# Turning token blocks through DRAM and VectorE in three stages, and dealing PSUM banks anew in a fourth

## The chip, the cores and the metric

One core of a Trainium2 chip runs the whole program. The metric is the device time of one execution in microseconds (us); the time of a kernel is the median of its runs.

## The reference

A decoder of two layers on x, 16 blocks of 128 tokens by 512 features, in float32. Each of the six parts is followed by an add and a layer norm:

```python
x = ln(x + attention(x))               # layer 0: 16 heads of 32, 4 key heads, rotary, softmax
x = ln(x + cross_attention(x, ctx))    # layer 0: low-rank queries and keys, context of 128 x 128 a block
x = ln(x + ffn(x))                     # layer 0: (sigmoid(x w1) * (x w2)) w3, weights cut to -1, 0, 1
x = ln(x + decay_attention(x))         # layer 1: scores times a decay, no softmax
x = ln(x + cross_attention_1(x, ctx))  # layer 1: softmax with a causal mask
x = ln(x + experts(x))                 # layer 1: 2 of 8 experts a token, and a shared one
```

A projection `x @ w` needs the tokens with their features on the partitions, that is, each block of x turned from (128 tokens, 512 features) to four squares of (128 features, 128 tokens). How the blocks are turned is what this case is about.

## The kernel before

All of x lies in SBUF as 16 tiles `x[b]` of 128 tokens by 512 features. The stages run one after the other; each goes through the blocks in four groups of four (`GB` = 4, `NG` = 4), and projects a whole group of 512 tokens at a time from a turned tile `xT` (128 features x 4 x 512 tokens).

The kernel deals with eight banks of PSUM, each large enough for 128 x 512 float32. `psum.share(mm=..., sc=..., ...)` shares them out by name for a stage, and `bank("mm", ...)` takes the next one of that name; a bank is free again when the last reader of its tile is done.

Before the change a block is turned in one way only in these stages: four TensorE transposes into a `mm` bank (`transpose_x`, records L127), and one copy out of it by ScalarE (L128). The FFN has its own form of it (L663), since it splits the turned block into a high and a low part, `xh` by ScalarE (L664) and `xl` by VectorE (L665).

- **First attention** (`attend` with its `prepare`, `score`, `value`). While group g is attended, the tasks of `prepare(g + 1)` are dealt in parts (`Share`) between the softmax pieces: four `turn`s, 20 projection matmuls, the values, and for g >= 2 a `folds` task that multiplies two heads' weights of the next stage together, out of a tile `raw` loaded from DRAM (two buffers). For g = 4 four more folds follow, of which the first can start when an earlier fold has freed its `raw`.
- **Cross-attention of layer 0** (`context`, `project`, `Heads`; banks mm=2, sc=4, av=2). 32 steps, one for each block and half of the heads. A step takes two `sc` banks for its scores (L563); VectorE finds the maximum (L186), ScalarE takes Exp with eight instructions (L191), GpSimd scales. Then the probabilities are turned by way of DRAM: VectorE's transpose turns 32 x 32 squares (L580), SP writes the tile to DRAM (L584) and fetches it in four DMAs that set the squares in place (L587). Two steps later `out` multiplies with `mT` into one `mm` bank, `po` (L605), which VectorE adds to x (L610). At a group's start `context` turns context and tokens (`pk` L531, `tr` L127), and `project` makes `qT` and `kT` (L546, L549), all through `mm`. Between the steps VectorE also sums and cuts the FFN's weights (`piece`, L470, L497, L499).
- **FFN** (`inputs`, then 11 steps f for each group; banks mm=2, sc=3, pt=2, av=1). A step is 16 matmuls into `pa` and `pb` (L687), a sigmoid (L692), a product `ht` on VectorE (L694), its high part `hh` (L696) and low part `hl` (L698). One task of the list `todo` is run ahead of each step but the first: in group 0 the cuts of the third weight's last pieces, then the next group's blocks to turn.
- **Decay attention** (banks mm=2, sc=4, av=2). A group's four blocks are turned, 8 x 4 projection matmuls follow (L775), the values (L783), and then the blocks go through a pipeline of three stages: scores (L799), values (L814), output (L148).

The order of instructions on each engine is settled when the program is built: a scheduler reckons with costs and takes, of what is ready, what was written first. `keep_in_program_order` pins an instruction behind everything that was written before it for its engine. A queue then runs in that order, and an instruction that waits holds all behind it; this is so for SP, which issues nearly all DMAs, too. Two buffers of a tag (`bufs=2`) let the writer run one tile ahead of the reader.

Of the kernel before, what the change touches and what calls it, by code (L numbers as in the profile page):

```python
# [12 lines left out]
F32 = mybir.dt.float32  # L13
F32R = mybir.dt.float32r
AF = mybir.ActivationFunctionType
ALU = mybir.AluOpType
AX = mybir.AxisListType

P = 128
# [26 lines left out]
def decoder_kernel(ctx: ExitStack, tc: tile.TileContext, a: dict, out: bass.AP):  # L46
# [25 lines left out]
    def bank(tag, shape, name):  # L72
        return psum.pool.tile(shape, F32, tag=tag, name=name, bufs=psum.banks[tag])
# [18 lines left out]
    def load_x(b0, b1):  # L92
        for b in range(b0, b1):
            nc.sync.dma_start(x[b], a["x"][b])
# [28 lines left out]
    def transpose_x(xT, b, at):  # L123

        tr = bank("mm", [P, KC, P], "tr")
        for k in range(KC):
            nc.tensor.transpose(tr[:, k, :], x[b][:, k * P : (k + 1) * P], ident)  # L127
        nc.scalar.copy(xT[:, :, at : at + P], tr)  # L128

    def chain(tasks, name, pairs, then):  # L130

# [179 lines left out]
    with tc.tile_pool(name="p1", bufs=1) as p1:  # L311
# [47 lines left out]
                    nc.vector.tensor_tensor(br, br, b2, ALU.add)  # L359

        load_x(GB, NB)
        LATE = H // 2 - 2
        nc.sync.dma_start(wkr, a["l0x_wkr"])
        hd = DC // 2
# [30 lines left out]
        def prepare(g):  # L395
            if g == NG:
                room = p1.tile([P, KC, TG], F32, tag="xT", name="room")
                ct, t2 = (room[:, n].rearrange("p (b d) -> p b d", d=DC) for n in range(2))
                return [(0, rotate(0, ct, kvr0, t2))] + folds(2, LATE)
            xT = p1.tile([P, KC, TG], F32, tag="xT", name="xT")  # L400
            qkT = p1.tile([P, 5, TG], F32, tag="qkT", name="qkT", bufs=2)
            v = p1.tile([P, GB, P], F32, tag="v", name="v", bufs=2)
            groups[g] = qkT, v
            tasks = []

            def turn(i):
                transpose_x(xT, g * GB + i, i * P)
                nc.gpsimd.tensor_tensor(x[g * GB + i], x[g * GB + i], bo, ALU.add)

            tasks += [(0.64, lambda i=i: turn(i)) for i in range(GB)]  # L410
            for c in range(5):
                chain(
                    tasks, "pq", [(wr[:, k, c * P : (c + 1) * P], xT[:, k, :]) for k in range(KC)],
                    lambda pq, c=c: nc.scalar.activation(qkT[:, c, :], pq, AF.Identity, bias=br[:, c : c + 1]),  # L414
                )
            got = {}

            def values_in(i):
                if i == 0:
                    got["pv"] = bank("pt" if g == 0 else "mm", [P, GB, P], "pv")  # L420
                for k in range(KC):
                    nc.tensor.matmul(
                        got["pv"][:, i, :], lhsT=xT[:, k, i * P : (i + 1) * P], rhs=wv[:, k, :],
                        start=(k == 0), stop=(k == KC - 1),
                    )
                if i == GB - 1:
                    nc.vector.tensor_tensor(v, got["pv"], bc(bv, GB), ALU.add)

            vals = [(0.93, lambda i=i: values_in(i)) for i in range(GB)]
            if g == 0:  # L430
                tasks = [t for pair in zip(tasks, vals) for t in pair] + tasks[GB:]
            else:
                tasks += vals
            return tasks + (folds(g - 2, g - 1) if g >= 2 else [])

# [63 lines left out]


    with tc.tile_pool(name="p2", bufs=1, reuse_waits="tile") as p2:
        psum.share(mm=2, sc=4, av=2)


        tern = Ternary(p2)
# [145 lines left out]
    with tc.tile_pool(name="p3", bufs=1) as p3:  # L653
        w1, w2 = (tern.w[n].rearrange("p (k f) -> p k f", k=KC) for n in range(2))
        def inputs(g):
            xh = p3.tile([P, KC, TG], F32R, tag="xh", name="xh", bufs=2)
            xl = p3.tile([P, KC, TG], F32R, tag="xl", name="xl", bufs=2)

            def one(i):
                at = slice(i * P, (i + 1) * P)  # L660
                tr = bank("mm", [P, KC, P], "tr")
                for k in range(KC):
                    nc.tensor.transpose(tr[:, k, :], x[g * GB + i][:, k * P : (k + 1) * P], ident)  # L663
                nc.scalar.copy(xh[:, :, at], tr)  # L664
                nc.vector.tensor_tensor(xl[:, :, at], tr, xh[:, :, at], ALU.subtract)  # L665
            return (xh, xl), [lambda i=i: one(i) for i in range(GB)]

        xs, todo = inputs(0)
        for run in todo:
# [4 lines left out]
        for g in range(NG):  # L674
# [2 lines left out]
                coming, more = inputs(g + 1)  # L677
                todo += more
            for f in range(NF0):
                if f and todo:  # L680
                    todo.pop(0)()
                pa = bank("sc", [P, TG], "pa")
                pb = bank("pt", [P, TG], "pb")
                for dst, wt in ((pa, w1), (pb, w2)):
                    for k in range(KC):
                        for n in range(2):
                            nc.tensor.matmul(  # L687
                                dst, lhsT=wt[:, k, f * P : (f + 1) * P], rhs=xs[n][:, k, :],
                                start=(k == 0 and n == 0), stop=(k == KC - 1 and n == 1),
                            )  # L690
                sg = p3.tile([P, TG], F32, tag="sg", name="sg", bufs=2)
                nc.scalar.activation(sg, pa, AF.Sigmoid)  # L692
                ht = p3.tile([P, TG], F32, tag="ht", name="ht", bufs=2)
                nc.vector.tensor_tensor(ht, sg, pb, ALU.mult)  # L694
                hh = p3.tile([P, TG], F32R, tag="hh", name="hh", bufs=NF0 + 1)
                nc.scalar.copy(hh, ht)  # L696
                hl = p3.tile([P, TG], F32R, tag="hl", name="hl", bufs=NF0 + 1)
                nc.gpsimd.tensor_tensor(hl, ht, hh, ALU.subtract)  # L698
                hs.append((hh, hl))
# [26 lines left out]
    with tc.tile_pool(name="p4", bufs=1) as p4:  # L726
# [28 lines left out]


        pipe = Pipeline((0, 1, 2))
        for g in range(NG):
            xT = p4.tile([P, KC, TG], F32, tag="xT", name="xT", bufs=2)
            for i in range(GB):  # L760
                transpose_x(xT, g * GB + i, i * P)
                nc.gpsimd.tensor_tensor(x[g * GB + i], x[g * GB + i], bo4, ALU.add)
            if g == 0:
                for j in range(4):
                    dj = p4.tile([P, 4, P], F32, tag=f"dec{j}", name=f"dec{j}")
                    for c in range(4):
                        h = 4 * c + j
                        nc.scalar.activation(dj[:, c, :], diff, AF.Exp, scale=nsl[:, h : h + 1])
                    nc.gpsimd.tensor_tensor(dj, dj, bc(maskT, 4), ALU.mult)
                    dec.append(dj)  # L770
            qkT = p4.tile([P, 8, TG], F32, tag="qkT", name="qkT", bufs=2)
            for c in range(8):
                pq = bank("mm", [P, TG], "pq")
                for k in range(KC):
                    nc.tensor.matmul(  # L775
                        pq, lhsT=wq4[k // 2][:, k % 2, c * P : (c + 1) * P], rhs=xT[:, k, :], start=(k == 0), stop=(k == KC - 1)
                    )
                nc.scalar.activation(qkT[:, c, :], pq, AF.Identity, bias=bcol[:, c : c + 1])
            vs = []
            for i in range(GB):  # L780
                pv = bank("mm", [P, D], "pv")
# [5 lines left out]
                v = p4.tile([P, D], F32, tag="v", name="v", bufs=6)  # L787
                nc.vector.tensor_tensor(v, pv, bv4, ALU.add)
                vs.append(v)
            for i in range(GB):  # L790
                toks = slice(i * P, (i + 1) * P)
                mine = {}

# [626 lines left out]
```

## Time and profile before

| | |
|---|---|
| median of 3 runs | 2102.32 us (2101.36 to 2102.72) |
| the profiled execution | 2102.39 us |
| its span, first to last instruction | 2100.6 us |
| TensorE busy | 2038.5 us (97%) |
| VectorE, ScalarE, GpSimd busy | 853.1, 625.0, 646.8 us |
| mean DMA rate | 113 GB/s over the span |

The profile is of one execution. In its rows PE is TensorE's matmul, PEld its weight load, DVE VectorE, ACT ScalarE, POOL GpSimd and SP SyncE, whose only work is issuing DMAs. L127 is line 127 of the kernel. A row of the waits has who waited, for whom, the total in us, the number of waits and the longest. A row of the timeline has the start, the duration, the instruction and, in brackets, the idle time before it. A float32 matmul of 512 columns shows as two records, a transpose as one. A matmul's record lasts longer than the distance to the next one's start, since matmuls are pipelined.

### The profile page before, as it was taken

What the parts mean: (1) busy time and instruction counts of PE and PEld (TensorE: products, weight loads), DVE (VectorE), ACT (ScalarE), POOL (GpSimd) and SP (SyncE); (2) the same over time, 40 slices, a digit from 0 to 9 for tenths busy, and PEclk for the clock granted to TensorE, in tenths of its full rate; (3) what the DMA queues carried; (4) which work ended last, traced back from release to release, by engine and by line L of the source; (5) the groups of instructions that cost most, each with busy time, mean ns of one, the idle gap of its engine ahead of it and who ended that gap; (6) DMA issues with size and microseconds to landing.
All of it is one profiled execution on the core that took longest, in us unless ns stands there. A gap on an engine that the chain in (4) does not pass through costs nothing. (4 is left out here: it accounts for less than half of the span.)

```text
span 2100.6 us, 25187 instructions
## 1 busy us (share of the span) xinstructions
PE 2038.5 (97%) x9221; PEld 1125.7 (54%) x9221; DVE 853.1 (41%) x1728; ACT 625.0 (30%) x2103; POOL 646.8 (31%) x674
## 2 busy tenths in 40 slices
PE   8999989999999999999999999999899999999997
PEld 5555544444444458888555444555544455545552
DVE  4667732444554243222123213777731122232324
ACT  3655532333333222222211111766632200000002
POOL 5555530111211122223223123455613212222223
PEclk9999999999999999999999999999999999999999
DMA  6001231334432220000300008600003379999974
GB/s 230 1 35 40 106 129 54 99 124 125 136 119 78 70 85 1 1 1 35 120 1 1 1 6 248 244 22 21 26 19 126 122 218 305 295 295 305 289 236 165
DMA packets 117067, 238.19 MB, mean 113 GB/s; under 512 B 28752, under 2 KB 73168, under 8 KB 110288
## 3 DMA queue, kind: packets, MB, share of 16 engines
q1 hardware_dynamic: 102048, 129.72, 19.1%
q0 software_dynamic: 13792, 105.55, 15.3%
q8 instruction: 73, 1.20, 0.2%
q10 hardware_dynamic: 1104, 1.31, 0.2%
q14 instruction: 50, 0.41, 0.1%
HBM read 172.25 MB, written 64.30 MB: 113 GB/s over the span
## 5 line engine op out<-in xcount | busy, mean ns | idle before, releaser
L198 POOL TENSOR_TENSOR p<-p,rs 128x512 f32<-128x512 f32 x192 | 200.0, 1043 | 504.8 <-DVE rs L197 500.0
L605 PE MATMUL po<-mT,cc 128*128 128x512 f32 x512 | 232.5, 602 | 3.7 <-ACT cc L598 3.7
L191 ACT ACTIVATE p<-t,nmx 128x128 f32<-128x128 f32 x512 | 198.5, 390 | 34.6 <-POOL p L198 8.8
L605 PEld LDWEIGHTS po<-mT,cc 128*128 128x128 f32 x512 | 95.5, 191 | 117.7 <-issue 107.4
L191 ACT ACTIVATE p<-sc,nmx 128x128 f32<-128x128 f32 x256 | 90.0, 372 | 113.7 <-DVE nmx L186 107.9
L546 PE MATMUL pq<-xT,wqr 128*128 128x512 f32 x256 | 117.9, 602 | 3.0 <-ACT xT L128 3.0
L114 POOL TENSOR_SCALAR ve<-mv 128x1 f32<-128x1 f32 x80 | 18.1, 226 | 324.3 <-DVE mv L112 312.3
L148 PE MATMUL po<-wo,oT 128*128 128x512 f32 x256 | 116.8, 599 | 0.4 <-ACT qkT L414 0.4
L1163 ACT ACTIVATE rsg<-rg 128x352 f32<-128x352 f32 x39 | 18.1, 463 | 331.2 <-PE rg L1158 331.2
L775 PE MATMUL pq<-xT,wq 128*128 128x512 f32 x256 | 110.9, 594 | 1.0 <-ACT xT L128 0.7
L1158 PE MATMUL rg<-ew,xsT 128*128 128x352 f32 x312 | 100.5, 465 | 11.3 <-DMA ew<-in_l1f_w_dram,which 10.6
L1179 PE MATMUL ry<-ew,ractT 128*128 128x512 f32 (+1 forms) x234 | 106.9, 592 | 0.0
L121 POOL TENSOR_SCALAR x<-x,mv,rstd 128x512 f32<-128x512 f32 x48 | 100.6, 2095 | 4.5
L1158 PE MATMUL ru<-ew,xsT 128*128 128x352 f32 x312 | 98.7, 459 | 0.0
L1129 POOL DMA_INDIRECT ew<-in_l1f_w_dram,which x39 | 38.0, 975 | 190.7 <-PE ry L1179 167.9
L191 ACT ACTIVATION_READ_ACCUMULATOR p<-t,nmx 128x1 f32 x512 | 96.2, 188 | 0.0
L698 POOL TENSOR_TENSOR hl<-ht,hh 128x512 fp32r<-128x512 f32 x44 | 60.4, 1372 | 114.9 <-ACT hh L696 114.9
L205 DVE COPY pT<-pt 128x512 f32<-128x512 f32 x128 | 86.5, 679 | 18.0 <-PE pt L203 18.0
L1189 POOL DMA_INDIRECT sums<-ry,place x39 | 62.0, 1590 | 96.2 <-DMA sums<-ry,place 43.9
L203 PEld LDWEIGHTS pt<-ident,p 128*128 128x128 f32 x512 | 59.8, 141 | 53.8 <-issue 44.8
L1041 PE MATMUL pg<-xT,sw_gu 128*128 128x512 f32 x192 | 86.5, 593 | 0.0
L186 DVE TENSOR_REDUCE nmx<-t 128x4 f32<-128x512 f32 x128 | 83.8, 675 | 0.8
(231 smaller groups left out, 3617.7 us busy)
## 6 DMA issues: line engine op xcount, KB each, us to landing
piece<-in_l0f_w_dram SPq DMA_DIRECT2D x48, 352.0 KB
away<-sq SPq DMA_DIRECT2D x32, 512.0 KB
pT<-away SPq DMA_DIRECT2D x128, 128.0 KB
raw<-in_l0x_raw_dram SPq DMA_DIRECT2D x8, 1728.0 KB
slots_x<-zero SPq DMA_DIRECT2D x1, 10023.0 KB
sums<-zero SPq DMA_DIRECT2D x1, 9984.0 KB
xs<-slots_x SPq DMA_DIRECT2D x156, 64.0 KB
sums<-x SPq DMA_DIRECT2D x16, 256.0 KB
```

The lines of the kernel that those rows point to most:

```text
L121: engine.tensor_scalar(x[b], x[b], mean, rstd, ALU.subtract, ALU.mult)
L148: nc.tensor.matmul(po, lhsT=oT[:, c, :], rhs=wo[:, c, :], start=(c == 0), stop=(c == KC - 1))
L186: nc.vector.tensor_reduce(nmx, src, axis=AX.X, op=ALU.max, negate=True)
L191: nc.scalar.activation(self.p[:, j, :], src[:, j, :], AF.Exp, bias=nmx[:, j : j + 1], accum_out=self.sm[:, j : j + 1])
L198: nc.gpsimd.tensor_tensor(self.p, self.p, spread(rs, P), ALU.mult)
L205: nc.vector.tensor_copy(self.pT, pt)
L546: nc.tensor.matmul(pq, lhsT=wqr[:, k, cols], rhs=xT[:, k, :], start=(k == 0), stop=(k == KC - 1))
L605: nc.tensor.matmul(self.po, lhsT=self.cc[:, 4 * par + j, :], rhs=mT[h], start=(par == 0 and j == 0), stop=(par == 1 and j == 3),)
L775: nc.tensor.matmul(pq, lhsT=wq4[k // 2][:, k % 2, c * P : (c + 1) * P], rhs=xT[:, k, :], start=(k == 0), stop=(k == KC - 1))
L1041: nc.tensor.matmul(dst, lhsT=sw_gu[:, k, at : at + P], rhs=xTs[g][:, k, :], start=(k == 0), stop=(k == KC - 1),)
L1158: nc.tensor.matmul(dst, lhsT=self.xT[:, k, :], rhs=gu[:, k, off : off + FE], start=(k == 0), stop=(k == KC - 1),)
L1179: nc.tensor.matmul(po, lhsT=self.actT[:mw, m_, :], rhs=dn[:mw, m_, :], start=(m_ == 0), stop=(m_ == 2))
```

## The change

A new class `Turn` turns a block without TensorE. `send` lets ScalarE regroup x[b] by squares of 32 features into `xp` and writes it to a DRAM tile `turned`; `fetch` brings it back in four DMAs so that the 32 x 32 squares stand where they belong; `back` lets VectorE transpose the squares into `xT`.

- In the first attention, groups 2 and 3: no `send`; eight DMAs, after the loads of x, regroup the input from DRAM to DRAM in runs of 32 floats. The folds of these groups now come ahead of the projections, with the four turns (at cost 0) between them.
- In the FFN, groups 1 to 3: sends and backs go into `todo` in a fixed order, and the list is spread over the steps, so that in group 0 more than one task can fall to a step.
- In the decay attention, groups 1 to 3: two blocks of the next group are sent during the projections, two at the first attention step; they come back at the first and the third. `xT` has one buffer in place of two.
- In the cross-attention of layer 0: four `mm` banks in place of two, two `sc` banks in place of four.

```diff
+    turned = dram.tile([NB, P, D], F32, tag="turned", name="turned")
+    QP = P // 4
+
+    class Turn:
+        def __init__(self, b):
+            self.b = b
+
+        def send(self, pool, tag="xp"):
+            xp = pool.tile([P, 4, KC, QP], F32, tag=tag, name="xp")
+            nc.scalar.copy(xp, x[self.b].rearrange("p (k q a) -> p q k a", k=KC, q=4))
+            nc.sync.dma_start(turned[self.b], xp.rearrange("p q k a -> p (q k a)"))
+
+        def fetch(self, pool, tag="x2", bufs=1):
+            self.x2 = pool.tile([P, 4, P], F32, tag=tag, name="x2", bufs=bufs)
+            rows = turned[self.b].rearrange("(t r) (q f) -> q r t f", r=QP, q=4)
+            for q in range(4):
+                nc.sync.dma_start(self.x2[q * QP : (q + 1) * QP], rows[q])
+
+        def back(self, xT):
+            tc.keep_in_program_order(nc.vector.transpose(
+                xT.rearrange("p k (t r) -> p t k r", r=QP), self.x2.rearrange("p t (k a) -> p t k a", k=KC)
+            ))
@@ first attention, after the loads of x
         load_x(GB, NB)
+        for g in range(2, NG):
+            blocks = slice(g * GB, (g + 1) * GB)
+            for k in range(KC):
+                nc.sync.dma_start(
+                    turned[blocks].rearrange("n p (q k a) -> (n p) q k a", q=4, k=KC)[:, :, k, :],
+                    a["x"][blocks].rearrange("n p (k q a) -> (n p) k q a", q=4, k=KC)[:, k],
+                )
@@ first attention, prepare(g)
             def turn(i):
-                transpose_x(xT, g * GB + i, i * P)
+                if g < 2:
+                    transpose_x(xT, g * GB + i, i * P)
+                else:
+                    mine = Turn(g * GB + i)
+                    mine.fetch(p1, bufs=3)
+                    mine.back(xT[:, :, i * P : (i + 1) * P])
                 nc.gpsimd.tensor_tensor(x[g * GB + i], x[g * GB + i], bo, ALU.add)
 
-            tasks += [(0.64, lambda i=i: turn(i)) for i in range(GB)]
+            tasks += [(0.0 if g >= 2 else 0.64, lambda i=i: turn(i)) for i in range(GB)]
...
-            return tasks + (folds(g - 2, g - 1) if g >= 2 else [])
+            first = folds(g - 2, g - 1) if g >= 2 else []
+            for i in range(GB):
+                first.insert(2 * i, tasks[i])
+            return first + tasks[GB:]
@@ cross-attention of layer 0
-        psum.share(mm=2, sc=4, av=2)
+        psum.share(mm=4, sc=2, av=2)
@@ FFN, inputs(g)
+            turns = [Turn(g * GB + i) for i in range(GB)]
+
+            def sent(i):
+                turns[i].send(p3)
+                turns[i].fetch(p3, bufs=2)
+
             def one(i):
                 at = slice(i * P, (i + 1) * P)
-                tr = bank("mm", [P, KC, P], "tr")
-                for k in range(KC):
-                    nc.tensor.transpose(tr[:, k, :], x[g * GB + i][:, k * P : (k + 1) * P], ident)
+                if g == 0:
+                    tr = bank("mm", [P, KC, P], "tr")
+                    for k in range(KC):
+                        nc.tensor.transpose(tr[:, k, :], x[i][:, k * P : (k + 1) * P], ident)
+                else:
+                    tr = p3.tile([P, KC, P], F32, tag="xT", name="xT")
+                    turns[i].back(tr)
                 nc.scalar.copy(xh[:, :, at], tr)
                 nc.vector.tensor_tensor(xl[:, :, at], tr, xh[:, :, at], ALU.subtract)
-            return (xh, xl), [lambda i=i: one(i) for i in range(GB)]
+
+            if g == 0:
+                return (xh, xl), [lambda i=i: one(i) for i in range(GB)]
+            order = [(sent, 0), (sent, 1), (one, 0), (sent, 2), (one, 1), (sent, 3), (one, 2), (None, 0), (one, 3)]
+            return (xh, xl), [lambda f=f, i=i: f and f(i) for f, i in order]
@@ FFN, the steps of a group
-                if f and todo:
+                for _ in range(-(-len(todo) // (NF0 - f)) if f else 0):
                     todo.pop(0)()
@@ decay attention
+        coming = []
+
+        def send4(b):
+            coming.append(Turn(b))
+            coming[-1].send(p4)
+            coming[-1].fetch(p4, bufs=2)
+            nc.gpsimd.tensor_tensor(x[b], x[b], bo4, ALU.add)
+
         for g in range(NG):
-            xT = p4.tile([P, KC, TG], F32, tag="xT", name="xT", bufs=2)
-            for i in range(GB):
-                transpose_x(xT, g * GB + i, i * P)
-                nc.gpsimd.tensor_tensor(x[g * GB + i], x[g * GB + i], bo4, ALU.add)
             if g == 0:
+                xT = p4.tile([P, KC, TG], F32, tag="xT", name="xT")
+                for i in range(GB):
+                    transpose_x(xT, i, i * P)
+                    nc.gpsimd.tensor_tensor(x[i], x[i], bo4, ALU.add)
...
                 nc.scalar.activation(qkT[:, c, :], pq, AF.Identity, bias=bcol[:, c : c + 1])
+                if c in (2, 4) and g + 1 < NG:
+                    send4((g + 1) * GB + c // 2 - 1)
...
+            if g + 1 < NG:
+                xT = p4.tile([P, KC, TG], F32, tag="xT", name="xT")
             for i in range(GB):
+                if i in (0, 2) and g + 1 < NG:
+                    for n in (i, i + 1):
+                        coming.pop(0).back(xT[:, :, n * P : (n + 1) * P])
+                        if i == 0:
+                            send4((g + 1) * GB + 2 + n)
```

## The prediction

> **What bounds the kernel now.** I read the page first, then busy times by stage, then TensorE's waits, then the timeline at a few places. The page:
>
> ```profile
> PE 2038.5 (97%) x9221; PEld 1125.7 (54%) x9221; DVE 853.1 (41%) x1728; ACT 625.0 (30%) x2103; POOL 646.8 (31%) x674
> PE   8999989999999999999999999999899999999997
> DMA  6001231334432220000300008600003379999974
> ```
>
> TensorE is busy nearly everywhere; DMA is nearly idle in slices 2 to 4 (52 to 210 us) and in the FFN and decay stages. A busy TensorE can hide lost pitch, so I also ask for the four stages that the change touches (first attention, cross-attention, FFN, decay attention):
>
> ```profile
> 0.00:262.00 262.00, 251.90 (x1571) 146.87 (x1571) 167.93 (x337) 140.83 (x577) 144.10 (x147) 0.99 0.23 82
> 262.00:759.00 497.00, 483.94 (x1630) 228.08 (x1628) 203.39 (x381) 160.38 (x628) 93.66 (x109) 1.00 0.32 102
> 759.00:1013.70 254.70, 251.22 (x1124) 206.85 (x1123) 86.36 (x140) 63.04 (x105) 72.84 (x76) 0.99 0.07 24
> 1013.70:1286.00 272.30, 269.67 (x1599) 134.05 (x1598) 75.68 (x132) 46.30 (x81) 67.20 (x73) 1.00 0.14 35
> ```
>
> Columns: stretch, length, busy PE, weight load, DVE, ACT, POOL, granted clock, DMA share, GB/s. TensorE is at 96 to 99% in all four, VectorE at 64, 41, 34 and 28%. So work taken off TensorE counts in full, and VectorE has room. TensorE's waits, the rows that bear on the change:
>
> ```profile
> PE po L605 <- ACT cc L598: 3.7, 1, 3.7
> PE pq L546 <- ACT xT L128: 3.0, 4, 0.8
> PE tr L127 <- DVE x L610: 2.9, 2, 1.8
> PE av L593 <- DMA pT<-away: 1.6, 1, 1.6
> PE tr L127 <- ACT kvT L533: 0.5, 1, 0.5
> ```
>
> All five lie in cross-attention. In the third and fifth the transposes wait for a bank of `mm`, of which there are two there: one held by `po` until VectorE has added it to x (L610), one by `pk`.
>
> **What a transposed block costs TensorE.** FFN timeline:
>
> ```profile
> 907.63 0.39 PE L687 MATMUL pb<-xl,ffn_w 128*128 128x512 f32 x1
> 907.86 0.60 PE L663 MATMUL tr<-ident,x 128*128 128x128 f32 x4
> 908.22 0.48 PE L687 MATMUL pa<-xh,ffn_w 128*128 128x512 f32 x1
> 908.53 0.40 PE L687 MATMUL pa<-xl,ffn_w 128*128 128x512 f32 x1
> ```
>
> The FFN's matmuls start 0.226 us apart (907.63 to 907.86). With four transposes and one matmul between, 907.86 to 908.53 is 0.67, so the four cost 0.67 - 0.226 = 0.44 us. Elsewhere the same: four records last 0.60, one alone 0.272, so they start (0.60 - 0.272)/3 = 0.109 apart, 0.44 for four.
>
> **Transposes removed.** First attention, groups 2 and 3: 8 blocks. FFN, groups 1 to 3: 12. Decay, groups 1 to 3: 12. 32 x 0.44 = 14.1 us (3.5, 5.3, 5.3), all on the engine that sets the end. The small waits beside them (0.24 to 0.34 us at the first attention's group starts, some 0.1 per decay group) give another 0.5.
>
> **What replaces them.** On VectorE one `back` per block. The nearest rows are the same instruction on the same 128x512 tile, 711 ns at L580 and 697 ns at L1147: 0.70. First attention gets 8 x 0.70 = 5.6 us more on 168 of 262; the FFN 8.4 on 86 of 255; decay 8.4 on 76 of 272. The cover is VectorE's idle time; where it is gone, a `back` costs at most its 0.70. In the first attention the four stand in the first third of a group's share instead of being spread, with VectorE at 64%: I charge 0.5 us there (bounds 0 and 5.6).
>
> ScalarE: decay loses 12 copies out of PSUM (L128, 585 ns) and gains 12 copies into `xp` (the row of such a regrouping copy, L1108, has 618 ns): level. The first attention loses 8. The FFN gains 12 x 0.62 = 7.4 on 63 of 255. Free. `xh` and `xl` read SBUF in place of PSUM; L665 at 690 and L696 at 621 (SBUF to SBUF) say at most 0.03 each.
>
> DMA and SP: per block of FFN and decay one write of 256 KB and four fetches. The same pair in cross-attention:
>
> ```profile
> 412.26 0.34 SPq L584 DMA_DIRECT2D away<-sq  x1
> 414.97 1.74 SPq L587 DMA_DIRECT2D pT<-away  x4
> ```
>
> The write is answered 2.71 us after its issue, and the four fetches take 1.74 to issue. With a copy of 0.62 before and a landing that I bound by 1 and 2.7 (as long as the write), a trip takes 6.1 to 7.8 us. While SP waits for the write, everything behind it waits: in the FFN's group 0 the third weight's pieces. A FFN step is 16 x 0.226 = 3.6 us; groups 1 and 2 leave two steps (7.2) from send to `back`. Group 0 leaves one for its first block, but the copy needs only x, so it can run ahead; and `back` on VectorE holds `ht`, for which two `pb` banks give about 4 us of cover. In group 0 two `cut`s per step instead of one make 2 x (0.58 + 0.95) + 0.69 = 3.75 us of VectorE per 3.6 us step for three steps, and pieces 2.9 us from issue to use come two by two: `ht` falls some 2 us behind, inside that cover. I charge 1.0 for the FFN (bounds 0 and 4).
>
> Decay: blocks 0 and 1 of the next group leave during the projections, over 20 us before their `back`; blocks 2 and 3 have two attention steps (scores start 5.75 apart, 1127.15 and 1132.90), 11.5 us, for two trips that share one `xp`: 2 x 4.45 + 0.6 + 1 to 2.7 = 10.5 to 12.2. About even; 0 charged, bounds 0 and 3 x 0.7 = 2.
>
> DRAM to DRAM in the first attention: 8 copies on SP after the last x load (issued until 23.1 us), before `wkr`, the tables and the first two `raw`. See the second rival.
>
> **Banks in cross-attention.** With four `mm` banks the waits for a bank, 2.9 + 0.5, should go: 3.4 us. The 3.0 us in which `pq` waits for the last copy of xT stay: five ScalarE copies of 0.59 still follow one another. `sc` falls from four banks to two: scores of the next block wait for the Exp of this one. The steps are 10 us apart, and the closest case in the trace is this:
>
> ```profile
> 545.06 1.16 PE L563 MATMUL sc<-kT,qT 64*128 64x128 f32 x16
> 552.95 0.37 ACT L191 ACTIVATE p<-sc,nmx 128x128 f32<-128x128 f32 x1
> 553.22 0.48 PE L563 MATMUL sc<-kT,qT 64*128 64x128 f32 x2
> ```
>
> The last Exp ends at 553.32, 0.1 after the next scores start. In the other steps 0.7 to 5 us lie between, so two banks nearly suffice: 0 charged. At the start of the stage four blocks' scores are now done ahead, and ScalarE runs their Exps before the first `cc` (the 3.7 us wait); with two banks it could get to `cc` sooner. Bounds: 0 and a gain of 3.7 plus 1.7 (the granted clock is 0.51 for 3.5 us after that wait: 3.5 x 0.49). I take 0, since nothing shows the new order.
>
> **Sum.** -14.1 - 0.5 - 3.4 + 0.5 + 1.0 = -16.5. The profiled execution took 2102.39 us (span 2100.6), 0.07 from the median of the runs, so the same sum serves: 2102.4 - 16.5 = 2085.9, say 2086. Taking every bound for it (-14.1 - 0.5 - 3.4 - 3.0 - 5.4): 2076.
>
> **Rival 1: the squares come late.** Trips as long as their upper bound and no copy ahead: the FFN's first block 4.2 late, decay 2, and a wait that long is followed by a slow clock, 1.7: about 8 back, so 2094. For it: SP and VectorE keep their order, and one late block holds all behind. Against: x is ready long before. Chance 0.21, nearly all still faster.
>
> **Rival 2: the early copies hold up `raw`.** 2 MB in runs of 32 floats are 8 x 2048 = 16,384 pieces. By bytes, 4.2 MB read and written at the 410 GB/s of the stretch from 16 to 36 us take 10 us; at the mean of the hardware queue's packets (19.1% of 16 x 2100.6 us over 102,048 packets, 63 ns), 16,384 x 63/16 = 64 us. The loads before them end near 36, so they end between 46 and 100, and the first `raw` some 5 us later. The folds now come first in group 2, near 87 us, where the work of group 2 starts in the trace, and not at 136.9. At the upper end TensorE waits 105 - 87 = 18 us: 2104. I take the low end: the mean packet has 1,270 bytes, ten times these, and DMA is idle from 40 to 86 us. The Trainium skill ("DMA: Bandwidth & Descriptors", Specifications) speaks against such pieces: under 512 B a DMA engine reads, modifies and writes. By an estimate from it, twice the bytes' time, they would end near 56, which leaves the sum as it is; no row here shows 128-byte writes to DRAM. Chance 0.07, over half of it within the bound of no change.
>
> **Rival 3, slower: two score banks set the pace of cross-attention.** Of the 32 steps some 24 follow another block's scores directly. If the order, made for banks that free at a reckoned time, puts scores 1.2 us before the Exps are done, 24 x 1.2 = 29 us are lost: 2086 + 29 = 2115. It decides from 16.5/24 = 0.7 us a step. For it: the case above, 0.1 short, and VectorE's sums over the weights, which come between scores and Exp. Against: the median step has about 4 us to spare. Chance 0.09.
>
> **How the numbers follow.** Forecast 0.63 (2076 to 2092), rival 1 0.21 (2090 to 2099), rival 2 0.07, rival 3 0.09. A measurement of this kernel can tell about 0.2%, 4.2 us, from no change. Faster: 0.63 + 0.19 = 0.82; same: 0.02 + 0.04 = 0.06; slower: 0.03 + 0.09 = 0.12. The range 2075 to 2100 holds the forecast with its bounds and rival 1, and leaves out the other two.
>
> **What would show it.** L127 has 320 - 80 = 240 records and L663 16; VectorE has 32 more stream transposes of 0.70; FFN and decay shrink by 4 to 6 us each, first attention by 3, cross-attention by 3 to 4; no wait of `tr` on L610 is left in it. Wrong: waits of `pc` on a `raw` load near 87 us, of `sc` on Exp in cross-attention, or of `ht` on `piece` or on a fetched block.

## The result, and the profile after

The changed kernel takes 2084.76 us (median; 2083.01 to 2086.05) beside 2102.30 (2101.36 to 2102.72) of the kernel before: a ratio of 0.9908, interval 0.9894 to 0.9923. The forecast was 2086.0. The profiled execution took 2083.65 us, its span is 2081.9. The page of the kernel after:

```profile
PE 2024.5 (97%) x9093; PEld 1119.0 (54%) x9093; DVE 880.7 (42%) x1760; ACT 627.3 (30%) x2107; POOL 644.5 (31%) x674
PE   8999999999999999999999999999899999999997
DMA  9200331334432231001410028400004279999974
```

TensorE has 128 instructions fewer (9221 to 9093: 32 blocks of four transposes) and 14.0 us less busy time; VectorE has 32 more instructions and 27.6 us more; 32 `back`s at 0.695 us are 22.2 of them, and where the rest lies is told under FFN below. DMA, idle before in the slices of FFN and decay, now has a few tenths there. The same four stretches as in the prediction:

```profile
0.00:257.50 257.50, 247.31 (x1539) 142.16 (x1539) 172.01 (x345) 136.77 (x569) 144.27 (x147) 0.99 0.33 100
257.50:750.20 492.70, 485.18 (x1630) 233.86 (x1629) 203.65 (x381) 159.94 (x628) 93.71 (x109) 0.99 0.32 103
750.20:999.00 248.80, 245.32 (x1077) 202.17 (x1076) 102.62 (x153) 69.45 (x117) 69.88 (x76) 0.99 0.16 50
999.00:1265.10 266.10, 263.39 (x1551) 130.44 (x1550) 82.80 (x144) 46.55 (x81) 67.57 (x72) 0.99 0.21 60
```

VectorE (the fifth column) rose by 16 us in the FFN and 7 in decay, and TensorE is as full as before, in shorter stages. In the next table, as in what follows, a stage is measured between fixed records of TensorE (the first `pk` of each cross-attention, the last `po` of cross-attention and of the FFN, the first of the gate), in us:

| kernel | first attention | cross-attention, layer 0 | FFN | decay | cross-attention, layer 1 | the rest | span |
|---|---|---|---|---|---|---|---|
| before | 262.4 | 496.5 | 254.4 | 273.2 | 237.5 | 576.6 | 2100.6 |
| after | 257.9 | 492.1 | 248.5 | 267.1 | 239.2 | 577.0 | 2081.9 |
| after, profiled again (f_after) | 259.3 | 492.5 | 247.1 | 266.8 | 238.7 | 579.0 | 2083.4 |

The four stages that were touched give 4.5, 4.4, 5.9 and 6.1 us, 20.9 together; 1.7 is lost in layer 1's cross-attention and 0.5 after it, where nothing was changed. The groups of transposes and of VectorE's turned squares (line, engine, operation, count, then busy time and mean ns of one, then idle time before them):

```profile
L127 PE MATMUL tr<-ident,x 128*128 128x128 f32 x240 | 35.0, 286 | 12.0 <-DMA x<-in_x_dram 7.7 <-ACT xT L128 1.5 <-DVE x L653 1.2
L713 PE MATMUL tr<-ident,x 128*128 128x128 f32 x16 | 2.7, 315 | 2.8 <-DVE xl L718 2.0 <-DVE x L653 0.8
L153 DVE STREAM_TRANSPOSE xT<-x 128x512 f32<-128x512 f32 x32 | 21.8, 695 | 0.0
```

240, 16 and 32 records, and 695 ns for one `back`, all as forecast. TensorE's waits in cross-attention and the FFN (who waited, for whom, total, times, longest):

```profile
PE sc L606 <- ACT p L218: 3.1, 2, 2.3
PE pq L589 <- ACT xT L128: 2.9, 3, 1.2
...
PE tr L127 <- DVE x L653: 1.2, 2, 0.9
...
PE po L648 <- ACT cc L641: 0.2, 1, 0.2
```

Of the five waits shown before, `pq` is as it was; `tr` on x has fallen from 2.9 to 1.2; `po` on `cc` from 3.7 to 0.2; `av` on `pT` (1.6) and `tr` on `kvT` (0.5) are not among the rows any more. New is `sc` on the Exp, 3.1, at the start of the stage: the prediction had named waits of `sc` on Exp as a sign of being wrong, and had expected none of `tr` on x to be left.

### The profile page after: what moved, and what is told of

It reads as the page before. It is cut to its first block, busy times and chain, and to the rows that moved or that the text cites. A ratio compares the mean times of both kernels' runs of the same rounds, so it can differ in the third digit from the quotient of the medians.

```text
span 2081.9 us, 25292 instructions
## 1 busy us (share of the span) xinstructions
PE 2024.5 (97%) x9093; PEld 1119.0 (54%) x9093; DVE 880.7 (42%) x1760; ACT 627.3 (30%) x2107; POOL 644.5 (31%) x674
## 5 line engine op out<-in xcount | busy, mean ns | idle before, releaser
L218 ACT ACTIVATE p<-t,nmx 128x128 f32<-128x128 f32 x512 | 198.5, 389 | 34.1 <-POOL p L225 10.2
L755 POOL TENSOR_TENSOR hl<-ht,hh 128x512 fp32r<-128x512 f32 x44 | 57.4, 1305 | 112.0 <-ACT hh L753 112.0
L1239 DVE TENSOR_TENSOR ract<-rsg,ru 128x352 f32<-128x352 f32 x39 | 20.3, 521 | 154.7 <-issue 138.3
```

Source lines behind the costliest of these rows:

```text
L218: nc.scalar.activation(self.p[:, j, :], src[:, j, :], AF.Exp, bias=nmx[:, j : j + 1], accum_out=self.sm[:, j : j + 1])
```

## The experiments

The kernel before took 2102.3 to 2104.3 us (medians) in the different sessions, so each time is given with its ratio to the kernel before on the same chip and the interval of that ratio. Where a difference between stages is told, it is from the profiled executions, one for each kernel.

**Banks alone, and turning alone.** e_banks is the kernel before with the one line, e_turns the kernel after without it.

```diff
 # e_banks: on the kernel before      # e_turns: the reverse, on the kernel after
-        psum.share(mm=2, sc=4, av=2)
+        psum.share(mm=4, sc=2, av=2)
```

> The kernel before with one edit: in layer 0's cross-attention four mm banks and two score banks, nothing turned by DRAM. Theory A (TensorE's work and its waits for a bank set the time): the stage gets 4 us shorter as in the changed kernel (497 to 493), 2098 us, with the 3.7 us wait of po for cc gone and a new wait of some 3 us of the scores for Exp at the stage's start. Theory B (the stage got shorter only because the stage before it ends otherwise): no change, 2101 to 2103. Rival 3 of the prediction (two score banks set the pace): scores wait for Exp in many of the 32 steps and the stage gets longer than 500 us.

> The changed kernel with the banks of cross-attention as before (two mm, four score banks); the three stages are turned by DRAM. Theory A: 32 blocks at 0.44 us less on TensorE and the small waits beside them, 14 to 16 us off: 2086 to 2089 us, and with the run of the banks alone the two gains add up to the whole change of 17.5. Theory B (they lean on each other): less than 12 us off here.

e_banks: 2099.39 us, 0.9982 [0.9969, 0.9995]. Its cross-attention takes 492.0 us in place of 496.5. Its waits there:

```profile
PE sc L563 <- ACT p L191: 3.4, 3, 2.3
PE pq L546 <- ACT xT L128: 2.9, 3, 1.2
...
PE tr L127 <- DVE x L610: 1.2, 2, 0.9
```

They are those of the kernel after: four banks for projections bring the waits for a bank down, and two banks for scores put a wait of the scores on the Exp at the start, and nowhere else. Rival 3 is out: behind the first scores of the stage (297.6 to 301.9 us) no score waits longer than 0.01 us. e_turns: 2088.15 us, 0.9920 [0.9901, 0.9939]; its first attention and FFN are those of the kernel after (257.9 and 248.5). Its cross-attention, with the banks of before, takes 495.2, so between these two kernels the banks are worth 3 us, and 4.5 between before and e_banks. The two parts of the change stand by themselves: 0.2% and 0.8% make the 0.9 to 1.0% of the kernel after.

**Each stage's turning.** e_ffn and e_first are the kernel before with the change of one stage.

```diff
 # e_ffn: class Turn, and in inputs(g) and the FFN's steps
+            order = [(sent, 0), (sent, 1), (one, 0), (sent, 2), (one, 1), (sent, 3), (one, 2), (None, 0), (one, 3)]
+                for _ in range(-(-len(todo) // (NF0 - f)) if f else 0):
 # e_first: class Turn, the eight early copies, and in prepare(g) for g >= 2
+                    mine.fetch(p1, bufs=3)
+                    mine.back(xT[:, :, i * P : (i + 1) * P])
```

> The kernel before with the change of the FFN alone (groups 1 to 3 turned by way of DRAM and VectorE). Theory A (the transposes removed are worth 12 x 0.44 = 5.3 us and nothing is paid back; the FFN's part of the change stands by itself): FFN stage 254.4 to 248.5 to 249.1, the other stages as before, total 2096 to 2097.5, ratio 0.997 to 0.9977. Theory B (the prediction's charge of 1.0 us for the trips and the crowded tasks of group 0 is paid, and what was measured beyond it in the whole change came from the stage before): stage 250 or more, total 2098 or more. Below 248.5 neither would explain it, and a slow-clock stretch that moved out of the stage is to be looked for.

> The kernel before with the change of the first attention alone (groups 2 and 3). Theory A (8 x 0.44 = 3.5 us of transposes and 0.3 to 0.6 us of small waits go, up to 0.5 is paid back): stage 262.4 to 258.9 to 259.3, the rest as before, total 2098.8 to 2099.3. Theory B (part of the 4.5 us by which the stage shrank in the kernel after is a stretch of slow clock at its start that is 3.4 us shorter there, worth 1.7 us, and comes and goes with the build): stage 257.5 to 258 if that stretch near 42 us is 3.4 us long, 259 to 259.6 if it is 6.8; the length of the stretch tells which.

e_ffn: 2099.31 us, 0.9982 [0.9969, 0.9995]; its FFN takes 248.3 us in place of 254.4. That is 6.0 less, and just below what either theory allowed; of the total, 2099.3 is above A's 2096 to 2097.5, while the interval of the ratio holds A's 0.997 to 0.9977. No slow clock moved out of the stage: its stretch is 6.8 us long in both. By the starts of TensorE's instructions the transposes of the stage fell from 9.8 to 5.7 us with their waits, and the first matmuls of a step (`pa` of `xh` and `xl`), which stand beside the transposes, by 1.7: the 5.3 had the transposes and one matmul after them, and about 0.5 more lies in the next ones. The profiled execution is no shorter than that of before, since cross-attention took 2.5 us more, decay 1.9 and the stages behind the gate 3.4. In the first two there are stretches of slow clock that before has shorter (3.4 us at 306.5) or doesn't have:

```profile
303.50:310.50 7.00, 5.44 (x7) 2.34 (x8) 2.37 (x5) 2.00 (x8) 2.07 (x3) 0.51 0.68 208
624.50:628.00 3.50, 3.38 (x8) 2.14 (x9) 2.78 (x5) 1.39 (x4) 0.56 (x1) 0.51 0.08 32
1058.00:1065.00 7.00, 7.00 (x104) 5.59 (x101) 4.90 (x8) 0.73 (x2) 0.00 (x0) 0.51 0.01 2
```

The third number from the end is the granted clock. Nothing was changed in those two stages. e_first: 2100.33 us, 0.9992 [0.9979, 1.0004], which the times alone can't tell from no change; its first attention takes 258.1 in place of 262.4, 4.3 less. Theory B holds, to 0.1, for the stage: the slow stretch that starts near 42 us (40.3 to 47.1 before) is 3.4 us long in it as in the kernel after, and 6.8 in the second profile of the kernel after, whose stage is 259.3. e_ffn, which has the first attention of before, happens to have 3.4 us there too, and takes 260.9: at that length the change is worth 2.8 us. The decay attention's change was not run alone.

**Each `back` twice, and backs behind the scores.** e_double asks what VectorE's cover is worth, e_late whether `back` ahead of the scores delays decay.

```diff
 # e_double
+            for _ in range(2):
                 tc.keep_in_program_order(nc.vector.transpose(
 # e_late: decay, the block "if i in (0, 2) and g + 1 < NG: back ... send4" moved
 # from ahead of the scores of step i to behind them
```

> The changed kernel with each of the 32 backs done twice in a row, the second writing the same values: 32 x 0.70 = 22 us more of VectorE, and nothing else. Theory A (VectorE's idle time covers the backs): at most 2 us longer, and those where the backs stand ahead of the decay's products of scores. Theory B (VectorE's order passes a good part on to TensorE): 8 us or more longer, first in the first attention, where VectorE is 67% busy.

> The changed kernel, with the two backs at a step of the decay attention written behind the block's scores and not ahead of them. In the changed kernel VectorE does two backs (1.29 us) at 1044.49 before the first product of scores and decay; TensorE then waits 1.47 us (0.83 before), and from 1048.8 on the granted clock is 0.5 for 6.8 us. Theory A (that order brings the slow stretch about): the wait goes back to 0.8, the stretch is gone, 3 us less, 2082 us. Theory B (the slow stretch comes by chance of its window): the same time as the changed kernel within 1 us, and a stretch there or not.

e_double: 2088.17 us, 0.9921 [0.9905, 0.9936], with 22 us more on VectorE. Its span is 2.7 to 4.3 us above those of the kernel after: an eighth to a fifth of the added work comes out at the end, between the two theories. It comes out in decay, which takes 271.7 us (+4.6), and in the first attention, which takes 260.3, 2.4 more than the kernel after with a slow stretch of the same 3.4 us; FFN and cross-attention take what they took. In decay the slow stretch is 10.2 us long in place of 6.8, so only 1.5 of the 4.6 is the longer wait. The rows that grew, from 1.5 in decay and from less than 0.2 in the first attention:

```profile
PE sc L874 <- DVE sT L881: 3.0, 1, 3.0
```
```profile
PE pq L165 <- DVE xT L154: 1.5, 2, 0.8
...
PE pg L332 <- ACT mT L326: 1.2, 2, 0.6
```

e_late: 2083.94 us, 0.9904 [0.9886, 0.9922], no different from the kernel after. The wait of `sc` on `sT` is what it was before the change (0.8), so it was the pair of `back`s that had made it 1.5; but the slow stretch at the start of decay stayed (1048.1 to 1054.9), so that wait had not made the stretch. Decay takes 266.5 us in place of 266.8 to 267.1: this term was worth 0.4 to 0.6. Theory B holds.

**Three and three banks.**

```diff
-        psum.share(mm=4, sc=2, av=2)
+        psum.share(mm=3, sc=3, av=2)
```

> The kernel after, with three banks for projections and three for scores in layer 0's cross-attention, in place of four and two. Theory A (the 3.1 us in which the scores of the stage's start wait for Exp come from having two score banks, and the 3.4 us of bank waits that went away came from having two banks of the other kind): with three of each the score wait falls below 1 us, at most 1 us of bank waits comes back, and the stage is 490 to 492.5, the total within 2 us of the kernel after. Theory B (TensorE starts early in the stage whatever the banks, and waits for whatever ends last there, ScalarE's Exps and copies): the score wait goes, but another wait of 2.5 to 4 us takes its place at the start of the stage, on the copy cc as in the kernel before, and the stage is 492 to 494.

e_three: 2083.72 us, 0.9907 [0.9885, 0.9929]. Cross-attention takes 490.2 us, 1.9 less than after; its waits:

```profile
PE pq L589 <- ACT xT L128: 2.4, 3, 0.8
...
PE tr L127 <- DVE x L653: 2.1, 2, 1.3
PE sc L606 <- ACT p L218: 1.7, 2, 1.4
```

The score wait is 1.7 where A expected less than 1, and the bank wait is back by 0.9. Of A the direction and the stage's time hold, and no wait on `cc` took its place (0.2, as in the kernel after), so B falls. The gain in the sum, less than 2 us, is not told by the times; the slow stretch at the stage's start is 6.8 us long in place of 10.2, and what it gives is part of the 1.9.

**The early copies four times over.**

```diff
-        for g in range(2, NG):
+        for g in [2, 3] * 4:
             blocks = slice(g * GB, (g + 1) * GB)
```

> The kernel after, with the eight DRAM-to-DRAM copies of the first attention issued four times over (8 MB in 65,536 packets of 128 bytes in place of 16,384). It tests the price and the deciding point of the second rival: copies that hold up raw, the weights of the folds. Theory A (packets of 128 bytes take what they took, so that 2 MB need some 22 us, from 24 to 46 us; loads behind them wait): the copies end near 24 + 4 x 22 = 112, the first raw is in SBUF a few us later, and TensorE, which wants it at 85.7 us, waits 25 to 32 us; the first attention goes from 258 to 283 to 290 and the total to 2108 to 2116. Theory B (only the issue counts, 14.7 us for eight copies on SP, 59 for 32, and later loads run beside the copies on the DMA engines): raw is issued near 85 us and comes a few us late; the stage grows by 2 to 10 us and the total stays below 2095.

e_copies: 2091.71 us, 0.9943 [0.9925, 0.9961]; the first attention takes 266.3 us, 7 to 8 more than in the two profiles of after. SP's queue, the DMA share (second number from the end) with its rate while nothing but copies ran, and TensorE's wait:

```profile
23.00 55.99 SPq L392 DMA_DIRECT2D turned<-in_x_dram  x32
```
```profile
47.00:82.00 35.00, 34.58 (x207) 19.65 (x206) 20.84 (x44) 21.30 (x91) 13.27 (x13) 1.00 1.00 154
```
```profile
PE pc L310 <- DMA raw<-in_l0x_raw_dram: 5.6, 1, 5.6
```

The size is B's and the cause is neither's: issue takes 56 us, but the DMA engines are full all the while (1.00) at 154 GB/s, so the pieces set the pace and issue follows. 2.1 MB at 154 GB/s are 13.6 us. My 22 us for A had the last loads of x in them. The wait of 5.6 is followed by 6.9 us of slow clock (90.0 to 96.9), worth half of that, and both make 9.0. So rival 2's mechanism is real and was far off: with one set, SP issues the first `raw` at 40.9 us, for a use at 85.7. In e_copies it was there 10 us after its issue (81.7 to 91.7); by an estimate from these figures, 13.6 us a set, two more sets would still have been in time.

**Two steps further.** f_cross turns groups 1 to 3 of layer 0's cross-attention, f_last groups 2 and 3 of layer 1's in the same way; f_both has both and e_late; f_after is the kernel after beside them.

```diff
 # f_cross: the next group's four blocks, one send and one back a step, over the second half
+                    if half == 1:
+                        if i == 0:
+                            ready.append(p2.tile([P, KC, TG], F32, tag="xT", name="xT"))
+                        back2(i)
+                    if (half, i) == (0, 3) or (half == 1 and i < 3):
+                        send2((g + 1) * GB + (i + 1) % GB)
 # f_last: groups 2 and 3; values of the context first, a back and a send behind each, then pq
+                    tasks.append((0.0, lambda i=i: back5(i)))
+                    if i < 3:
+                        tasks.append((0.0, lambda i=i: send5(i + 1)))
```

> The changed kernel once more, unaltered, as the measure for the three beside it on the same chip: 0.991 of the kernel before, 17 to 20 us less.

> The changed kernel, with layer 0's cross-attention turned by DRAM too in groups 1 to 3: 12 blocks, one at a time through the tiles of the context's rotation (which moves two steps ahead), each back at a step of the second half of the group before. Theory A: 12 x 0.44 = 5.3 us of TensorE, and the waits around the transposes at three group starts (in the changed kernel 1.2 for x of L653 and some 2 for the last copy of xT) go: 6 to 8 us less than the changed kernel. Theory B (VectorE, in which a back waits for its fetch, holds up the maxima before the Exps, and two score banks pass it on to TensorE): less than 3 us, and new waits of the scores for Exp.

> The changed kernel, with layer 1's cross-attention turned by DRAM too in groups 2 and 3: 8 blocks, one at a time, the context's projections ahead of them. Theory A: 8 x 0.44 = 3.5 us less than the changed kernel, and the 0.3 to 0.4 waits at the two group starts. Theory B (VectorE is 67% and ScalarE 60% busy there, and a wait for a fetched block on VectorE holds up the softmax): no gain or a loss of 1 to 4 us, with waits of TensorE for p or pT in its place.

> Both of these and the decay attention's backs behind the scores, on the changed kernel. Theory A (all of it is TensorE's work, so the gains add): 9 to 12 us less than the changed kernel, 0.986 of the kernel before. Theory B: less than the better of the two alone.

f_after: 2081.63 us, 0.9897 [0.9882, 0.9913]. f_cross: 2085.16 us, 0.9914 [0.9896, 0.9933]: no gain, though 48 transposes are gone. Theory A is out; the size is B's, but the new waits are not those of the scores. Its stage is 1.1 us shorter than in f_after; the waits there:

```profile
PE pq L601 <- DVE xT L153: 5.9, 3, 2.5
...
PE po L660 <- ACT cc L653: 2.2, 2, 1.2
...
PE pq L601 <- ACT xT L128: 0.9, 1, 0.9
```

The last block of a group comes back 2 us late in each of three groups. The transposes and the waits of and for them (`tr`, and `pq` on ScalarE's last copy) took 9.2 us less, and the new waits in front of `pq` and `po` cost 8 us: a trip through DRAM is worth it only where the block leaves early enough, and here there was one buffer and one trip at a time.

f_last: 2092.28 us, 0.9938 [0.9918, 0.9959], slower than the kernel after, by more than either theory had and without B's waits. Its stage takes 252.4 us in place of 238.7 in f_after, while none of its waits is longer than there (0.9 at most). By the starts of TensorE's instructions the transposes gave 3.7 us; the scores (32 rows each) took 7.3 more, the projections `pq` 4.5 more and the products with `v` 3.0 more. In the kernel after, projections stand between these small matmuls; in f_last they gather at the end of a group, and in the profiled execution, the longest of six (2084.1 to 2097.2), they start there at half clock:

```profile
1372.60:1379.40 6.80, 6.80 (x23) 3.31 (x22) 4.93 (x10) 3.28 (x16) 2.08 (x2) 0.50 0.14 41
1434.00:1440.80 6.80, 6.80 (x23) 3.39 (x23) 5.16 (x10) 3.34 (x17) 2.08 (x2) 0.50 0.00 0
```

f_both: 2091.52 us, 0.9944 [0.9927, 0.9961], the loss of f_last, as its theory B has it. It has this stage as f_last has it, but without those two stretches, and takes 246.8 us for it: the scores took 6.6 more than in f_after, `pq` no more. So the edit costs this stage 8 us without them, and 5.6 more come with the two stretches in f_last. The edit puts the projections in another order and turns the blocks through DRAM at once; that the order is what costs is likely, since the small matmuls grew and no wait for a block did, but the two were not tried apart. No version tried is faster than the kernel after by more than the intervals.

## Why the prediction was right

**Stages at equal lengths of slow clock.** In most profiles each of these stages has a stretch at a granted clock of 0.50 to 0.51, and its length differs between profiles, also where the stage is the same in both. So a stage is compared here between profiles with a stretch of the same length in it (us):

| stage, length of its stretch | turned by TensorE | turned through DRAM | less |
|---|---|---|---|
| first attention, 6.8 | 262.4, 262.1 (before, e_banks) | 259.3, 259.4 (f_after, e_three) | 2.7 to 3.1 |
| first attention, 3.4 | 260.9 (e_ffn) | 257.9, 258.1 (after, e_first) | 2.8 to 3.0 |
| FFN, 6.8 | 254.4, 254.3 (before, e_first) | 248.5, 248.3 (after, e_ffn) | 5.8 to 6.1 |
| FFN, 3.4 | 252.9 (e_banks) | 247.1 (f_after) | 5.8 |
| decay, 6.8 | 275.1 (e_ffn) | 267.1, 266.8 (after, f_after) | 8.0 to 8.3 |
| decay, 3.4 | 273.6 (e_banks) | 265.6 (e_turns) | 8.0 |

The 4.5 us of the first attention hold about 1.5 of slow clock, and the 6.1 of decay are 8 less 2 of slow clock that before doesn't have.

**The transposes** (forecast: 14.1 and 0.5 for small waits). The mechanism was right, and the term too small by 3 us. By the starts of TensorE's instructions, the first attention gave 3.6 us (forecast 3.5); the FFN 4.3 for the transposes and 1.6 for matmuls beside them, 5.9 (5.3); decay 6.4 for the transposes and 1.6 for the products with `v` beside them (5.3 and 0.3). In decay, from one transpose to the next lie 0.11 us, but between a transpose and such a product 0.17 to 0.20, and a block's 32 products take 1.55 us beside transposes and 1.01 without. So 0.44 a block, measured in the FFN's densest place, is a lower bound elsewhere: with the matmuls beside them the stages give 0.45, 0.49 and 0.67.

**VectorE's cover** (0.5 in the first attention, bounds 0 and 5.6). The stage gained 2.7 to 3.1 where its transposes gave 3.6, so about 0.7 came back, which is near the charge. Of it 0.2 lies in waits: `pt` waits 0.7 for GpSimd in a row that before doesn't have, and 0.2 in place of 0.7 for VectorE. The rest is spread over how far apart the projections and the first groups' transposes start; that VectorE's order makes it so is not shown. e_double shows where the cover is thin: decay's first step, at which scores wait for `sT` behind a pair of `back`s, and the first attention.

**FFN** (1.0, bounds 0 and 4). Not paid: the only waits of the stage are those of its start and of group 0's first transposes (0.7, 2.0 and 0.8), which are the same before and after. Rival 1 has no place in it. One reading behind this term was wrong all the same. For `xl`, a VectorE instruction, the prediction took the time of L696, which is ScalarE's, and expected 0.03 us more from reading SBUF; it takes 0.54 more:

```profile
L665 DVE TENSOR_TENSOR xl<-tr,xh 128x512 fp32r<-128x512 f32 x16 | 11.0, 690 | 4.2 <-ACT xh L664 4.2
L718 DVE TENSOR_TENSOR xl<-xT,xh 128x512 fp32r<-128x512 f32 x12 | 14.8, 1234 | 9.6 <-ACT xh L717 9.6
```

For 12 blocks that is 6.5 us more of VectorE, nearly as much as the 8.4 of the `back`s. VectorE was busy for 34% of this stage before, and no wait of TensorE grew; how it would go in a stage with less room was not tried.

**Decay** (0, bounds 0 and 2). Blocks sent late came back in time. What was missed is the wait of `sc` on `sT` in step 0, where the pair of `back`s stands ahead of the scores' multiplication by the decay on VectorE:

```profile
1044.49 1.29 DVE L153 STREAM_TRANSPOSE xT<-x 128x512 f32<-128x512 f32 x2
1045.70 2.45 DVE L880 TENSOR_TENSOR sT<-sc,dec 128x512 f32<-128x512 f32 x4
1046.41 3.37 PE L873 MATMUL sc<-qkT 32*128 32x128 f32 x32 [1.47 <-DVE sT L880]
```

The wait was 0.8 before and is 1.5 now, and e_late takes it back to 0.8.

**Banks** (3.4; nothing for two score banks; bounds 0 and a gain of 5.4 at the start). The stage gave 4.4 (3 between e_turns and the kernel after), and the terms were not those of the sum. Of the 2.9 and 0.5 for banks, 2.2 went: `tr` on x stays at 1.2. The 3.7 of `po` on `cc` and the 1.6 of `av` on `pT`, for which nothing was booked, went nearly whole, as the upper bound had it for the first. By the starts of TensorE's instructions 1.0 more of small waits of `tr` went, and the projections, transposes and turns of the context stand 3.6 closer. Against this, 3.1 came of four blocks' scores in two banks waiting for the Exps, and the scores lie 4.7 further apart:

```profile
290.25 0.94 PE L606 MATMUL sc<-kT,qT 64*128 64x128 f32 x12
293.50 3.46 PE L606 MATMUL sc<-kT,qT 64*128 64x128 f32 x16 [2.31 <-ACT p L218]
297.75 3.61 PE L606 MATMUL sc<-kT,qT 64*128 64x128 f32 x16 [0.78 <-ACT p L218]
```

Twelve scores take 0.94 us, the next sixteen 3.46 and 3.61. The clock is slow from 294.4 to 304.7 us, 6.8 us longer than before in this place; the scores start 0.21 us apart in it and 0.11 just ahead of it. This length goes with the score banks: the stretch at the start of the stage is 10.2 or 13.6 us long in all nine profiles with two of them, 6.8 with three, and 3.4 (once 6.8) in the four with four. So the step "two banks nearly suffice" holds for the steps, and was wrong at the start of the stage. That the sum came out near is luck: gains of about 10 us were not booked, nor were losses of about 8.

**Rival 2.** The low end was right: in the kernel after the 16,384 pieces start between 25.5 and 41.1 us. The rate (last number) is near that of the pieces alone up to 40 us and rises behind it, when larger packets follow them; `raw` was issued at 40.9.

```profile
36.00:40.00 4.00, 3.74 (x39) 3.09 (x36) 3.91 (x8) 3.11 (x13) 4.00 (x4) 1.00 0.98 149
40.00:42.00 2.00, 1.49 (x12) 1.10 (x10) 1.93 (x5) 2.00 (x11) 2.00 (x3) 0.96 1.16 279
```

At the 13.6 us that e_copies shows for 2 MB, the copies lie between "by bytes" (10) and twice that, the estimate from the Trainium skill ("DMA: Bandwidth & Descriptors", Specifications).

**The rest.** 2.2 us were lost in stages without an edit, and no step of the sum has that. 1.7 of them are a slow stretch at 1297.9 to 1301.4 us (in layer 1's cross-attention, which takes 237.5 in the four profiles without such a stretch and, where it is not edited, 238.7 to 239.2 with one):

```profile
1298.00:1301.40 3.40, 3.40 (x4) 1.51 (x5) 2.28 (x5) 3.40 (x17) 1.24 (x2) 0.51 1.05 410
```

The stage of the experts (from its first `rg` to its last `ry`) varied from 353.3 to 362.8 us over the profiles here, with the same instructions in it. So the agreement to 1.2 us is in part luck: it is better than the kernel can be measured, and better than the steps. The touched stages gave 20.9 for a forecast of 16.5, and about 2 were lost elsewhere.

## What to carry to other kernels

A block that is turned on an idle engine and by way of DRAM is worth what its transposes cost on the engine that sets the end, if it leaves two steps ahead; measure it by the starts of the instructions, count the matmuls that stand beside them, and compare stages only where the slow clock in them is equally long. Doubling the replaced work (e_double) and multiplying its transfers (e_copies) show at once where its cover ends, which a profile without waits can't show. A change of order among projections, or of banks, can cost as much as was to be gained (f_last, as far as it is the order there, and the start of cross-attention), and the cost shows in pitch (how far apart instructions start) and clock before it shows in waits.

## What the runs showed of the hardware

**The slow clock comes in lengths of 3.4 us, and moves with the build.** In all profiles the stretches at half clock, but for the last one at the end, are 3.4, 6.8, 10.2 or 13.6 us long. The kernel before has three of them outside the last few us (17 us in all), the kernel after five (31 us). Matmuls of 512 columns lose half of such a stretch: two `pk` take 2.07 us in it and 1.02 outside. The attention matmuls of decay, with 32 rows or columns, lose less: beside the 6.8 us of stretch at its start, the scores and products of two blocks take 9.3 us by their starts in the kernel after and 9.2 in e_ffn, without the waits, and 7.2 before, so about 2 of 6.8 us. The Trainium skill ("TensorE: Matmul & The Clock Gate", Part 1) has a free-running window of about 3.4 us and a slow clock after a window of idling; the lengths agree. No such window is seen ahead of this stretch: in e_late, TensorE had waited 0.8 us at most in the stage, was busy for 3.40 and 2.57 us of the two times 3.40 us ahead of the stretch, and for all 6.80 of 6.80 us in it.

```profile
1048.20:1055.00 6.80, 6.80 (x96) 5.82 (x99) 4.47 (x8) 0.81 (x2) 1.26 (x1) 0.51 0.38 116
```

What decides whether a wait of 1 to 2 us is followed by one such length or two, or by none, these runs leave open.

**One instruction of VectorE takes longer by the time that GpSimd runs beside it.** The twelve `xl` that read two SBUF tiles (L718) take 0.84 to 1.37 us in the kernel after. GpSimd's `hl` (L755) runs during 0.29 us of the shortest, 0.82 of the longest and 0.71 or 0.72 of the other ten, and each time about 0.55 us is left; the four that read PSUM take 0.68 to 0.69. Whether other instructions of the two engines hold each other up in this way was not looked at.

**Short pieces are cheaper than the mean packet suggests.** A packet of 128 bytes takes 13 ns in e_copies (median of 67,584, of which 65,536 are those between two places in DRAM; over 16 engines they are 53 us, beside the 56 of the issue), where the hardware queue's mean before the change was 63 ns. For its bytes it is dear: 512 bytes take 27.
